# Convolution weights shared between VectorE and GpSimd, and a convolution that begins one tile later in the first image

## The chip, the cores and the metric

The kernel runs on one core of one Trainium2 chip. The metric is the device time of one execution in microseconds (us). Five engines work side by side, each through its own queue in order: TensorE (PE in the profile; its weight loads are PEld), VectorE (DVE), ScalarE (ACT), GpSimd (POOL) and SyncE (SP), which issues most of the transfers. SBUF is the on-chip memory, PSUM the memory into which TensorE accumulates.

## What is computed

Two layers on `x` of 2 images, 256 channels, 64x64, in float32. Layer 0 adds an 8-head attention over all 4096 positions to `x`. Layer 1, which the change touches, adds the following to its input:

```python
x = _gn(x)                                   # group normalisation
q, k, v = (1x1 convolutions of x by conv1, conv2, conv3)
ctx   = _sa(blockify(fq), blockify(fk), blockify(v))     # first attention: 64 tokens of a dilated 8x8 grid
feats = relu(scale * (lr_W @ ctx) + shift)
qx, kx, vx = (two-step 1x1 branches of feats, and sr_fv_w)
ctx2  = _sa(qx, kx, vx)                                  # second attention: 64 tokens of each 8x8 block
out_att = relu(scale * (sr_W @ ctx2) + shift)
f_conv  = fc_w applied over the 12 head slices of q, k, v    # 9 maps for each of 64 head channels
out_conv = grouped 3x3 convolution of f_conv with dep_w
return rate1 * out_att + rate2 * out_conv
```

`f_conv` and the grouped convolution are linear in `x`, so the kernel folds 1x1, mixing and 3x3 into one dense 3x3 convolution from 256 to 256 channels. Its weights depend on the inputs and are made on the chip, once, during the first image.

## The kernel before, in words

The images go one after the other. For each: statistics and projections of layer 0 (`project0`), its attention (`attention0`, some 950 us), the first attention of layer 1 (`layer1_first`) and the second attention together with the convolution (`layer1_second`). Each of the last two runs over NT = 8 tiles of 512 positions.

**Weights of the 3x3 (`conv_weights`, L760 to L840).** It is called at the end of `layer1_first` in the first image, and its instructions are filled in between those of the first attention's tiles. Small factors `weff` come first (L788 to L808). Then, for each half m of the output channels: 12 slices `wx` of 128x256 are loaded (L812); for each of the 9 taps, 12 products of a slice with a column of `weff` are added up (L813 to L820), all on VectorE; from the nine tap sums four rows of four (16 positions) are made by sums and differences (L824 to L831, the weight transform of Winograd's method); each of the 16 goes out to memory as `wf_kept` (L833). `wx`, the tap sums and the new rows lie in one buffer, and `new_cols` (L770) lies on the first eight slices of `wx`, so the second half's `wx` is loaded only when the first half is through. `fetch_conv_weights` (L845) reads all 16 positions back (L848), and in the first image turns each block on TensorE (L857), scales it (L860 on ScalarE, L862 on VectorE) and keeps the result for the second image (L863), which only loads it.

**Second attention and convolution (`layer1_second`, L1146 to L1242).** A tile has a branch for q (`fq1`, `fq2`: `phq_sr`, `prq_sr`), one for k (`phk_sr`, `prk_sr`), the group attention (`pvs_sr` values, `sp_sr` scores, the softmax L985 to L992 on VectorE and ScalarE, `at_sr` transposes, `bd` copies L1006, `pc_sr` context) and the result `res_sr`. The convolution has 16 steps, four for each of four strips of two tiles. A step is `conv_transform` on GpSimd (one instruction L884 and four L888, made one step ahead), 32 matmuls into `mm` (L898), and `conv_step`'s sums on VectorE into the tile's `x` (L904 to L925). TensorE's order is that of the program (`manual_schedule`). The program puts convolution steps at three places of a tile: between the branches, inside the softmax, and at the end of the tile. Before, tiles 0 and 1 have three steps, tiles 2 to 6 two, tile 7 none; `wf` is fetched in tile 0, after the branch for q. When the four steps of a strip are done, its two tiles' results are added up (L1237) and go out (L1240); only then is the `x` buffer free for the next image. The other engines' orders are set by a planner from its own estimates of costs, where the program's order is the priority; buffers of the pool `w4` (11 of them) are handed out the same way.

The choice of places in the code before:

```python
                if t == 0:
                    wf = fetch_conv_weights(b)
                if t + 1 < NT:
                    conv()
...
                if t < 2:
                    conv()
```

Of the kernel before, what the change touches and what calls it, by code (L numbers as in the profile page):

```python
# [17 lines left out]
P = 128  # L18
B, C, H, W = 2, 256, 64, 64
N = H * W  # L20
T = 512
NT = N // T
# [18 lines left out]
def direct_layers(ctx: ExitStack, tc: tile.TileContext, a: dict, out: bass.AP, bad: bass.AP):  # L41
# [3 lines left out]
    nc = tc.nc  # L45
# [13 lines left out]
    def w4(shape, name, dtype=F32):  # L59
        return work.tile(shape, dtype, tag="w4", name=name)  # L60
# [699 lines left out]
    def conv_weights():  # L760

        n_prep = 2 * 81 + 108 + 24 + 4 * 108
        place = vpool.tile([P, UW * C * KC], F32, tag="vw", name="prep")
        prep, rest = place[:, :n_prep], place[:, n_prep : n_prep + 27 * C].rearrange("p (i c) -> p i c", c=C)
        wx, taps, new_rows = rest[:, 0:12], rest[:, 12:21], rest[:, 21:27]
        new_cols = rest[:, 0:8].rearrange("p (r j) c -> p r j c", j=2)  # L770

        def part(at, n):
            return prep[:, at : at + n], at + n

        dep, at = part(0, 2 * 81)
        fcb, at = part(at, 108)
        bx, at = part(at, 24)
        weff, at = part(at, 2 * 108)
        tmp, at = part(at, 2 * 108)
        nc.gpsimd.dma_start(out=dep.rearrange("p (m f) -> p m f", m=2), in_=a["dep"].rearrange("(m p) f -> p m f", p=P))  # L780
        nc.gpsimd.dma_start(out=fcb, in_=a["fc"].partition_broadcast(P))
        nc.gpsimd.dma_start(out=bx.rearrange("p (m i) -> p m i", m=2), in_=a["bx"].rearrange("(m p) i -> p m i", p=P))
        dep = dep.rearrange("p (m o t) -> p m o t", m=2, o=9)
        fcb = fcb.rearrange("p (o i) -> p o i", o=9)
        bx = bx.rearrange("p (m i) -> p m i", m=2)
        weff = weff.rearrange("p (m i t) -> p m i t", m=2, i=12)
        tmp = tmp.rearrange("p (m i t) -> p m i t", m=2, i=12)
        for m in range(2):  # L788
            for o in range(9):
                dst = weff if o == 0 else tmp  # L790
                nc.vector.tensor_tensor(
                    dst[:, m],
                    dep[:, m, o, :].unsqueeze(1).to_broadcast([P, 12, 9]),
                    fcb[:, o, :].unsqueeze(2).to_broadcast([P, 12, 9]),
                    ALU.mult,
                )
                if o:
                    nc.vector.tensor_add(weff[:, m], weff[:, m], tmp[:, m])

        nc.vector.tensor_scalar(  # L800
            weff.rearrange("p m i t -> p (m i t)"), weff.rearrange("p m i t -> p (m i t)"), wts["rate2"], None, ALU.mult
        )
        btap = const.tile([P, 2, 9], F32, name="btap")
        for m in range(2):
            nc.vector.tensor_tensor(
                tmp[:, m], weff[:, m], bx[:, m, :].unsqueeze(2).to_broadcast([P, 12, 9]), ALU.mult
            )
            nc.vector.tensor_reduce(btap[:, m, :], tmp[:, m].rearrange("p i t -> p t i"), AX.X, ALU.add)  # L808

        for m in range(2):  # L810
            for q in range(3):
                nc.gpsimd.dma_start(out=wx[:, 4 * q : 4 * q + 4, :], in_=a["wx"][q, m].rearrange("i p c -> p i c"))  # L812
            for tap in range(9):  # L813
                acc = taps[:, tap, :]
                for i in range(12):
                    src, s = wx[:, i, :], weff[:, m, i, tap : tap + 1]
                    if i == 0:
                        nc.vector.tensor_scalar(acc, src, s, None, ALU.mult)
                    else:
                        nc.vector.scalar_tensor_tensor(acc, src, s, acc, ALU.mult, ALU.add)  # L820

            one, two = new_rows[:, 0:3, :], new_rows[:, 3:6, :]
            g = [taps[:, 3 * dy : 3 * dy + 3, :] for dy in range(3)]
            nc.vector.tensor_add(one, g[0], g[2])  # L824
            nc.vector.tensor_sub(two, one, g[1])
            nc.vector.tensor_add(one, one, g[1])
            for r, row in enumerate((g[0], one, two, g[2])):
                one, two = new_cols[:, r, 0, :], new_cols[:, r, 1, :]
                nc.vector.tensor_add(one, row[:, 0, :], row[:, 2, :])
                nc.vector.tensor_sub(two, one, row[:, 1, :])  # L830
                nc.vector.tensor_add(one, one, row[:, 1, :])  # L831
                for q, src in enumerate((row[:, 0, :], one, two, row[:, 2, :])):
                    nc.sync.dma_start(  # L833
                        out=wf_kept[:, :, 4 * r + q, m * P : (m + 1) * P], in_=src.rearrange("p (k c) -> p k c", k=KC)
                    )
        edges = const.tile([P, 2, 5], F32, name="edges")
        nc.vector.tensor_reduce(edges[:, :, 0], btap, AX.X, ALU.add)
        for e, three in enumerate((slice(0, 3), slice(6, 9), slice(0, 7, 3), slice(2, 9, 3))):
            nc.vector.tensor_reduce(edges[:, :, 1 + e], btap[:, :, three], AX.X, ALU.add, negate=True)
        return btap, edges  # L840
# [32 lines left out]
    def conv_transform(b, xp, s, q):  # L873

        def cols(d):
            return xp[:, :, 16 * s : 16 * s + 18, d : d + W - 1 : 2]

        def rows(d):
            return col[:, :, d : d + 15 : 2, :]

        terms = ((0, 2, False), (1, 2, True), (2, 1, False), (1, 3, False))
        col = cpool.tile([P, KC, 18, W // 2], F32, tag="col", name=f"col_{b}_{s}_{q}")
        one, two, plus = terms[q]
        (nc.gpsimd.tensor_add if plus else nc.gpsimd.tensor_sub)(col, cols(one), cols(two))  # L884
        v = [w4([P, 2, KC, STRIP], f"v_{b}_{s}_{q}_{n}") for n in range(2)]
        for r, (one, two, plus) in enumerate(terms):
            dst = v[r // 2][:, r % 2].rearrange("p k (i j) -> p k i j", j=W // 2)
            (nc.gpsimd.tensor_add if plus else nc.gpsimd.tensor_sub)(dst, rows(one), rows(two))  # L888
        return v
# [135 lines left out]
    def bn_relu(dst, src, col, m):  # L1025
        nc.scalar.activation(  # L1026
            dst, src, AF.Relu, bias=vecs[:, col + 2 + m : col + 3 + m], scale=vecs[:, col + m : col + m + 1]
        )


    def layer1_first(b, xts, put, check, st):
# [109 lines left out]
        if b == 0:  # L1141
            with tc.issue_after(done.ins):
                kept["bias"] = conv_weights()
        return feats, mean, rstd, shift

    def layer1_second(b, xts, feats, mean, rstd, shift, pacc):  # L1146
# [7 lines left out]
        def to_image(t):  # L1154
            for k in range(KC):
                nc.scalar.activation(  # L1156
                    xp[:, k, 1 + 8 * t : 9 + 8 * t, 1 : 1 + W], xts[t][:, k, :].rearrange("p (r w) -> p r w", w=W),
                    AF.Identity, bias=shift[:, k : k + 1], scale=rstd[:, k : k + 1],
                )
# [5 lines left out]
        ahead = {0: conv_transform(b, xp, *turns[0])}  # L1165
        done = 0

        def conv():
            nonlocal done
            if done + 1 < len(turns):  # L1170
                ahead[done + 1] = conv_transform(b, xp, *turns[done + 1])
            conv_step(b, xts, wf, ahead.pop(done), *turns[done], pacc)
            done += 1

        for t in range(NT):
# [25 lines left out]
            with tc.manual_schedule(engines={mybir.EngineType.PE}):  # L1201
                q = branch("fq1", "fq2", V_FQ1, V_FQ2, "q")
                for tt in {0: (3, 4)}.get(t, (t + 4,)):
                    if tt < NT:
                        to_image(tt)
                if t == 0:
                    wf = fetch_conv_weights(b)
                if t + 1 < NT:
                    conv()
                k = branch("fk1", "fk2", V_FK1, V_FK2, "k")  # L1210
                res = w4([P, KC, T], f"res_{nt}")

                def to_res(m, pc, res=res):

                    bn_relu(
                        res[:, m, :].rearrange("p (d o e) -> p o d e", d=8, o=8),
                        pc.rearrange("p (o d e) -> p o d e", o=8, d=8), V_SRW, m,
                    )

                parts = group_attention(  # L1220
                    nt, q, k, lambda c, w, f=f: f[c][:, w * P : (w + 1) * P], wts["fv"], to_res, apart=t + 1 < NT
                )
                next(parts)
                if t + 1 < NT:
                    conv()
                next(parts)
                next(parts, None)
                if t < 2:
                    conv()
            conv_edges(xts, t)  # L1230
            if b == B - 1 and t == 2:
# [594 lines left out]
```

## Time and profile before

| | value |
|---|---|
| time, median of 3 runs | 3211.84 us (3209.8 to 3215.32) |
| span of the profiled execution | 3211.4 us |
| TensorE busy | 3093.3 us, 96% |
| VectorE busy | 2487.2 us, 77% |
| ScalarE busy | 2316.5 us, 72% |
| GpSimd busy | 826.7 us, 26% |
| tap sums L820, 198 instructions on VectorE | 0.479 us each (median), from 1191.1 to 1313.8 us |
| first attention of the first image, TensorE | to some 1312 us |
| second attention and convolution of the first image | 1314 to some 1635 us |

A line of the timeline reads: start and length in us, engine, line of the code, operation, output and inputs, shape, count; in brackets, the idle time of the engine in front of it and what ended it. A group of equal instructions in a row stands as one line. Stages are read from the busy time of each engine in a stretch, given as engine busy time with the number of instructions.

### The profile page before, as it was taken

To read this page: it belongs to the slowest core of one execution; us is meant where nothing else is said; L and a number is where in the kernel's file an instruction comes from. 1 tells how busy PE (TensorE), PEld (TensorE's weight loads), DVE (VectorE), ACT (ScalarE), POOL (GpSimd) and SP (SyncE) were. 2 spreads that over 40 slices of the span, in tenths; PEclk is the share of its full clock that TensorE was granted. 3 is DMA by queue.
4 is the path that set the end of the run, shared out by engine and by line. 5 is a ranking of instruction groups with operands and counts; after the bars stand their busy time and mean duration, and the time that the engine had idled before them with its cause. 6 is when DMAs were issued, how large, how long until landed. Compare 5 with 4: busy or idle time off the path is not lost. (4 is left out here: it accounts for less than half of the span.)

```text
span 3211.4 us, 62287 instructions
## 1 busy us (share of the span) xinstructions
PE 3093.3 (96%) x24889; PEld 1838.3 (57%) x24889; DVE 2487.2 (77%) x3223; ACT 2316.5 (72%) x2371; POOL 826.7 (26%) x918
## 2 busy tenths in 40 slices
PE   7899999999999989699998999999999999899998
PEld 4455555555555545466754555555555555456766
DVE  4599998999999988664445899889999999724543
ACT  2699999999999963422235999999999999724222
POOL 2122222222222210344200222222222222104530
PEclk9999999999999999899999999999999999999999
DMA  7968789689786741310049696897887966500000
GB/s 255 258 132 170 157 156 182 138 166 175 155 178 130 149 101 50 131 33 27 27 174 270 129 183 139 159 173 144 172 168 159 191 130 129 143 3 11 20 14 21
DMA packets 242957, 425.73 MB, mean 133 GB/s; under 512 B 99009, under 2 KB 110361, under 8 KB 240225
## 3 DMA queue, kind: packets, MB, share of 16 engines
q0 software_dynamic: 96176, 240.42, 39.0%
q1 hardware_dynamic: 146480, 181.25, 21.0%
q8 instruction: 197, 3.23, 0.4%
q14 instruction: 104, 0.84, 0.1%
HBM read 118.78 MB, written 67.86 MB: 58 GB/s over the span
## 5 line engine op out<-in xcount | busy, mean ns | idle before, releaser
L519 DVE TENSOR_TENSOR e<-e,es 128x1024 f32<-128x1024 f32 (+1 forms) x952 | 1035.9, 1142 | 96.9 <-ACT es L472 95.1
L482 PE MATMUL av<-es,v 128*32 128x256 f32 (+1 forms) x9644 | 747.6, 390 | 0.0
L519 DVE TENSOR_TENSOR e<-e,v 128x1024 f32<-128x1024 f32 (+1 forms) x640 | 675.9, 1108 | 54.4 <-ACT v L472 53.0
L472 ACT ACTIVATE es<-sa 128x1536 f32<-128x1536 f32 (+1 forms) x444 | 635.6, 1432 | 94.9 <-PE sa L466 54.2
L466 PE MATMUL sa<-q,k 128*128 128x512 f32 x1736 | 561.2, 430 | 13.0 <-issue 4.5
L482 PE MATMUL av<-v 128*32 128x256 f32 (+1 forms) x6228 | 506.9, 389 | 0.0
L482 PEld LDWEIGHTS av<-es,v 128*32 128x32 f32 x9644 | 316.5, 109 | 299.7 <-issue 161.3
L466 PEld LDWEIGHTS sa<-q,k 128*128 128x128 f32 x1736 | 280.0, 188 | 296.5 <-issue 142.4
L466 PE MATMUL sc<-q,k 128*128 128x512 f32 x1180 | 372.3, 397 | 10.1 <-ACT es L472 8.5
L466 PE MATMUL sb<-q,k 128*128 128x512 f32 x1180 | 371.1, 395 | 1.3 <-ACT es L472 1.3
L482 PEld LDWEIGHTS av<-v 128*32 128x32 f32 x6228 | 216.7, 109 | 179.3 <-issue 82.2
L472 ACT ACTIVATE es<-sc 128x1024 f32<-128x1024 f32 x296 | 306.9, 1037 | 7.8 <-DMA v<-es 7.8
L472 ACT ACTIVATE v<-sc 128x1024 f32<-128x1024 f32 x294 | 304.8, 1037 | 1.0 <-DMA acc<-v 1.0
L472 ACT ACTIVATE es<-sb 128x1024 f32<-128x1024 f32 x296 | 302.1, 1021 | 4.0 <-DMA acc<-es 3.9
L472 ACT ACTIVATE v<-sb 128x1024 f32<-128x1024 f32 x294 | 300.0, 1020 | 0.5 <-DMA acc<-v 0.5
L466 PEld LDWEIGHTS sc<-q,k 128*128 128x128 f32 x1180 | 210.3, 188 | 82.4 <-ACT es L472 21.0
L466 PEld LDWEIGHTS sb<-q,k 128*128 128x128 f32 x1180 | 221.0, 188 | 56.1 <-ACT es L472 3.5
L472 ACT ACTIVATE v<-sa 128x1536 f32<-128x1536 f32 (+1 forms) x146 | 209.2, 1433 | 35.0 <-PE sa L466 14.9
L898 PE MATMUL mm<-v,wf 128*128 128x256 f32 x1024 | 229.5, 382 | 3.7 <-DVE z L907 3.7
L529 POOL DMA_DIRECT2D es<-es x118 | 101.2, 858 | 484.8 <-ACT es L472 438.2
L888 POOL TENSOR_TENSOR v<-col 128x512 f32<-128x512 f32 x128 | 162.7, 1300 | 237.2 <-PE sp_sr L977 82.3
L898 PEld LDWEIGHTS mm<-v,wf 128*128 128x128 f32 x1024 | 194.4, 191 | 38.4 <-issue 7.7
(243 smaller groups left out, 3254.2 us busy)
## 6 DMA issues: line engine op xcount, KB each, us to landing
acc<-es POOLq DMA_DIRECT2D x130, 512.0 KB, 6.4
acc<-v POOLq DMA_DIRECT2D x84, 512.0 KB, 6.3
es<-es POOLq DMA_DIRECT2D x138, 256.0 KB, 4.3
v<-es POOLq DMA_DIRECT2D x134, 256.0 KB, 5.1
k<-wk_halves SPq DMA_DIRECT2D x64, 512.0 KB
q<-wq_halves SPq DMA_DIRECT2D x256, 128.0 KB
v<-v POOLq DMA_DIRECT2D x90, 256.0 KB, 5.0
es<-v POOLq DMA_DIRECT2D x86, 256.0 KB, 4.0
```

What stands on the lines that cost most here:

```text
L466: nc.tensor.matmul(sc[:, i, :], held["k", g // 2][:, j * P : (j + 1) * P], held["q", g, u // 2][:, u % 2, :], start=True, stop=True,)
L472: nc.scalar.activation(dst, sc[:, i : i + m, :], AF.Exp, scale=SC0)
L482: nc.tensor.matmul(dst[HD0 * u : HD0 * u + HD0, n], lhs, rhs(u)[:, n], start=start, stop=stop)
L519: nc.vector.tensor_add(dst[:, s, :], dst[:, s, :], src)
L529: nc.gpsimd.dma_start(out=dst, in_=src, accum_op=ALU.add)
L888: (nc.gpsimd.tensor_add if plus else nc.gpsimd.tensor_sub)(dst, rows(one), rows(two))
L898: nc.tensor.matmul(mm[:, m, r, :], wf[:, k, 4 * r + q, m * P : (m + 1) * P], v[r // 2][:, r % 2, k, :], start=k == 0, stop=k == KC - 1,)
```

## The change

Two things. First, of the nine taps in a half, three (6, 7 and 8, the last row of the 3x3) are made on GpSimd, as a product into a scratch row and an addition for each of the 12 slices, where VectorE has one instruction for both; VectorE keeps six. The aim is to have both engines at the sums at once and the weights ready earlier. Second, in the first image no convolution step stands in tile 0 of the second attention; tiles 1 to 4 have three, tiles 5 and 6 two, and `wf` is fetched in tile 1. The aim is to give TensorE work of the attention while the weights aren't there. The second image keeps its order.

```diff
-            for tap in range(9):
-                acc = taps[:, tap, :]
+
+            for tap in (6, 0, 1, 7, 2, 3, 8, 4, 5):
+                acc, term = taps[:, tap, :], new_rows[:, 0, :]
                 for i in range(12):
                     src, s = wx[:, i, :], weff[:, m, i, tap : tap + 1]
-                    if i == 0:
+                    if tap >= 6:
+                        nc.gpsimd.tensor_mul(acc if i == 0 else term, src, s.to_broadcast([P, C]))
+                        if i:
+                            nc.gpsimd.tensor_add(acc, acc, term)
+                    elif i == 0:
                         nc.vector.tensor_scalar(acc, src, s, None, ALU.mult)
                     else:
                         nc.vector.scalar_tensor_tensor(acc, src, s, acc, ALU.mult, ALU.add)
...
+        steps = (0, 3, 3, 3, 3, 2, 2, 0) if b == 0 else (3, 3, 2, 2, 2, 2, 2, 0)
+
...
-                if t == 0:
+                if t == steps.index(max(steps)):
                     wf = fetch_conv_weights(b)
-                if t + 1 < NT:
+                if steps[t] > 0:
                     conv()
...
-                if t + 1 < NT:
+                if steps[t] > 1:
                     conv()
                 next(parts)
                 next(parts, None)
-                if t < 2:
+                if steps[t] > 2:
                     conv()
```

## The prediction

> **What bounds the kernel now.** I went from the busy time by slices (TensorE is at 96% over the span, with one hole near 1330 us) to the stages of that hole, then to the waits in it, then to the timelines of the three engines around it. Busy time by stage (length; PE, PEld, DVE, ACT, POOL; granted clock; DMA share, GB/s):
>
> ```profile
> 1190.60:1245.50 54.90, 54.49 (x311) 33.43 (x311) 51.41 (x142) 22.12 (x32) 0.00 (x0) 1.00 0.05 15
> 1260.40:1314.30 53.90, 50.77 (x278) 30.63 (x276) 51.61 (x136) 24.08 (x35) 0.79 (x6) 1.00 0.12 37
> 1314.30:1331.40 17.10, 7.40 (x16) 2.88 (x16) 17.06 (x12) 11.09 (x17) 15.34 (x10) 0.87 0.22 65
> 1331.40:1346.00 14.60, 0.00 (x1) 0.01 (x1) 0.00 (x0) 0.00 (x0) 10.19 (x7) 0.50 0.79 310
> ```
>
> The first two rows are the tap sums of output half m=0 and m=1: VectorE is nearly full, GpSimd idle, and TensorE is full with the first attention. Row three: VectorE ends the row and column sums (L824 to L831). Row four: the last piece goes out and all weights come back (L848), and TensorE does nothing. The timeline and the wait list of TensorE:
>
> ```profile
> 1318.51 3.70 PE L1194 MATMUL prq_sr<-hq_sr,wt_fq 128*128 128x512 f32 x8 [0.37 <-ACT hq_sr L1026]
> 1346.00 2.40 PE L857 MATMUL pw<-ident,wf 128*128 128x128 f32 x10 [23.79 <-DMA wf<-wf_kept]
> PE pw L857 <- DMA wf<-wf_kept: 23.8, 1, 23.8
> ```
>
> So in the first image TensorE, which sets the end, stands for 23.8 us on a chain: taps m=0, store, reload of `wx` (1245.5 to 1260.4; `new_cols` lies on `wx[0:8]`, so m=1 can't be loaded earlier), taps m=1, sums, store and load (14.6). A later end of that chain moves the rest of the kernel one for one.
>
> **What the skill says.** The Trainium skill, "SBUF — State Buffer", section "Who interferes with whom": VectorE and GpSimd share one port pair under an exclusive lock; a VectorE instruction with two SBUF inputs contends with a GpSimd instruction that reads SBUF, and the loser fully blocks. The tap step L820 has two SBUF inputs (`wx` and `acc`). The trace agrees, where the sums of m=1 meet the convolution's transforms:
>
> ```profile
> 1316.36 2.36 DVE L830 TENSOR_TENSOR prep<-prep 128x256 f32<-128x256 f32 x1
> 1318.65 2.03 DVE L826 TENSOR_TENSOR prep<-prep 128x768 f32<-128x768 f32 x1
> 1320.60 2.89 DVE L829 TENSOR_TENSOR prep<-prep 128x256 f32<-128x256 f32 x2
> 1327.10 4.26 DVE L831 TENSOR_TENSOR prep<-prep 128x256 f32<-128x256 f32 x3
> ```
>
> ```profile
> 1315.82 2.62 POOL L884 TENSOR_TENSOR col<-xp 128x1152 f32<-128x1152 f32 x1 [6.03 <-ACT xp L1156]
> 1318.52 6.09 POOL L888 TENSOR_TENSOR v<-col 128x512 f32<-128x512 f32 x4
> 1326.97 5.50 POOL L888 TENSOR_TENSOR v<-col 128x512 f32<-128x512 f32 x4
> 1368.01 4.93 POOL L888 TENSOR_TENSOR v<-col 128x512 f32<-128x512 f32 x4 [26.19 <-issue]
> ```
>
> A sum of 128x256 takes 0.42 us alone (one each 0.335) and here 1.4 to 2.4: exactly one gets through per GpSimd instruction. GpSimd loses little: four of 128x512 take 4.93 us alone (one each 1.22) and 5.50 beside VectorE, 0.15 more each, some 0.19 less than the VectorE instruction's own pace.
>
> **The change, part by part.**
>
> (a) *Taps 6, 7, 8 to GpSimd.* VectorE loses 3 x 12 instructions per half: 36 x 0.397 = 14.3 us (L820 repeats every 0.397 us: six take 2.46). GpSimd gains 3 x (12 products + 11 sums) = 69 instructions of 128x256 per half. None of that size is in the trace. From below: half of 1.22 is 0.61, and 2.6 cycles an element at 1.2 GHz ("GPSIMD Engine Reference", "3.1 Elementwise — side-by-side cycle accounting") give an estimate of 0.56. From above: the straight line through 512 elements (1.22) and 1152 (2.13, 2.2 from start to start) gives 0.84. I take 0.63: at 512 elements that page's rate gives 1.11, near the 1.22. Every product and sum reads SBUF, so it alternates with L820: a cycle is 0.63 - 0.19 + 0.40 = 0.84 us, in which each engine does one instruction.
>
> Half m=0: VectorE has 66 sums, 6 products and 4 normalisations (L992), 76 contending instructions. About 17% of its time goes to work of the first attention that doesn't contend (maximum, subtraction, sum, reciprocal, two copies: 2.0 us of each 16.0 us tile, and short waits); then GpSimd runs alone. GpSimd: (0.83/0.84 + 0.17/0.63) T = 69, T = 54.9 us. VectorE has done 54 by then; the other 22 take 22 x 0.397/0.83 = 10.4. Half m=0 takes 65.3 us instead of 54.9: **10.4 us longer**, although 14.3 us of VectorE's work is gone.
>
> Half m=1 starts at 1270.8. To 1309 the first attention is still there: 48 of GpSimd's 69; the other 21 take 17.6, to 1326.6. VectorE has then done 59 of 74; 15 and the 15 row and column sums are left. Now GpSimd, whose queue is in order, comes to the convolution's transforms (three turns of L884 and 4 x L888 and one more L884, as before: 16 instructions, 23.4 us alone, some 26 so). VectorE gets 16 through by 1352.6, the other 14 take 5.8: the chain ends at **1358.4, not 1331.4: D = 27 us later**. Store and load (14.6) stay.
>
> (b) *No convolution in tile 0 of the first image; `wf` fetched in tile 1.* TensorE's stay moves behind tile 0's second branch and attention and tile 1's first branch. That work, today after the wait: 7.0 (k branch from 1362.35), 3.0 (values, scores), 4.4 (transposes, values, context), 7.2 (q branch): 21.6 us, now done while it would stand. New: the softmax of tile 0 isn't hidden by a convolution step.
>
> ```profile
> 1371.04 1.15 PE L977 MATMUL sp_sr<-rk_sr,rq_sr 128*64 128x64 f32 x32
> 1372.12 7.17 PE L898 MATMUL mm<-v,wf 128*128 128x256 f32 x32
> 1379.13 0.38 PE L997 MATMUL at_sr<-ident,e_sr 128*128 128x128 f32 x2
> ```
>
> Scores end at 1372.2, VectorE is through with L992 at 1375.4: 3.3 us of standing. Without other waits TensorE would be ready for the weights at 1322.2 + 21.6 + 3.3 = 1347.1; they come at 1346 + D. For D over 1.1 the time is 3211.8 - 21.6 + D.
>
> (c) *Queues.* The softmax of tile 0 can land on VectorE behind blocked tap sums; even behind the last of them, 4 us of chain, 4.5 of TensorE and the 7.2 of the q branch end within 2 us of the weights' arrival (14.6 after it), so up to 2 us. The convolution steps number 16 as before; from tile 4 on the two orders have done the same number (12, 14, 16). Tiles 3 and 4 now have three steps where tiles 0 and 1 had them: 42 us of TensorE each against some 34 of VectorE, hidden. Three results instead of two are held to tile 2's first step, in 11 `w4` buffers: nothing to 2 us. In the first attention a softmax chain of 3.5 us grows to 7 with 8.1 of TensorE's work beside it: hidden or covered by the wait for the weights. The second image keeps its order: nothing.
>
> Sum: 3211.8 - 21.6 + 27.0 = 3217.2, say 3217 us.
>
> **Rivals.**
> 1. *GpSimd runs beside VectorE.* Then a half ends after 54.9 - 14.3 = 41 us on VectorE and 69 x 0.63 = 43 on GpSimd, the chain some 24 us earlier, and the weights are there before 1347: TensorE saves 23.8 - 3.3 and the slow clock of the transposes (10 take 2.40 at 1346, later 8 take 0.87: 2.6 us): 3189. For it: L820 never stands beside a GpSimd instruction in the trace. Against: L919, the same operation, does, and two of 128x128, 0.6 us alone, took 3.56 us at 1385.25, one for each GpSimd instruction. A milder form (cycle 0.75, GpSimd 0.56) gives D = 17 by the same steps: 3207.
> 2. *GpSimd at 0.84 alone, 1.05 in turn.* Half m=0 takes 80 us, GpSimd ends m=1 at 1356, the sums at 1385: D = 54, 3244, slower by 1%. For it: the straight line through two sizes. Against: those rows run over two and three dimensions, a tap is one flat row.
> 3. *Transforms put between the taps on GpSimd's queue* (the planner picks by its own estimates): up to 7 us a turn, 3224 to 3231. The taps come first in the program, which speaks against it.
>
> **How the numbers follow.** The alternation at 0.75 to 0.95 us a cycle: 0.5, 3207 to 3231, middle 3217. Rival 1 whole or in good part: 0.25, 3189 to 3205. Rivals 2 and 3: 0.25, 3224 to 3244. The range 3190 to 3242 leaves out the ends. Faster by over 0.2% (below 3205.4): rival 1 and the edge of the middle, 0.32. Within 0.2%: 0.27. Slower: 0.41.
>
> **What would show it.** L820 repeating at 0.8 to 0.9 us while GpSimd works, not 0.397; GpSimd's products at about 0.63; half m=0 ending near 1256; the sums near 1358; TensorE standing some 25 us before L857 with tile 0's attention ahead of it. Wrong, if L820 keeps 0.4 us, if the last sum ends before 1335, or if TensorE's stay is under 10 us.

## The result and the profile after

The changed kernel takes 3236.9 us (median of 4 runs, 3234.5 to 3238.3) where the kernel before, on the same chip, takes 3210.8: a ratio of 1.0078, with an interval of 1.006 to 1.0095. It is slower, by 0.8%. The profiled span is 3236.4 us, 25.0 over the 3211.4 of before.

Lines of the code have moved: a tap sum is now L825 on VectorE (L823 its first product), and L819 (product) and L821 (addition) on GpSimd; the softmax is L990 to L997, its transposes L1002, the `bd` copies L1011, the context L1020, the stores of the weights L838, the transposes of the weights L862.

Busy time by stage of the kernel after (length; PE, PEld, DVE, ACT, POOL with their counts; granted clock; DMA share, GB/s). The rows are GpSimd's taps of m=0, its taps of m=1, the last sums, and the way of the weights to memory and back:

```profile
1190.50:1245.20 54.70, 42.26 (x211) 24.25 (x212) 54.58 (x81) 14.53 (x21) 49.76 (x69) 0.84 0.03 9
1265.20:1320.60 55.40, 40.09 (x174) 22.60 (x172) 55.24 (x80) 11.84 (x18) 50.40 (x69) 0.85 0.05 16
1320.60:1332.60 12.00, 9.40 (x17) 3.45 (x17) 11.72 (x29) 3.15 (x6) 0.00 (x0) 0.72 0.33 93
1332.60:1347.20 14.60, 14.60 (x84) 9.15 (x84) 2.73 (x8) 5.79 (x9) 0.00 (x0) 1.00 0.87 332
```

In the last row the weights come in, at the time they came before (1347.2 against 1346.0), and TensorE is full and doesn't care. In the first two it is not: in the first it works 42.3 us of 54.7, where before it was full to 0.4 us, and it gets 211 matmuls done where it had done 311. The timeline of TensorE, and its waits from 1190 to 1360 us:

```profile
1229.55 0.69 PE L1002 MATMUL at_lr<-ident,e_lr 128*128 128x128 f32 x2 [5.75 <-DVE e_lr L997]
1240.01 3.47 PE L1020 MATMUL pc_lr<-bd,vs_lr 128*128 128x128 f32 x16 [3.95 <-DVE bd L1011]
...
1299.14 0.69 PE L1002 MATMUL at_lr<-ident,e_lr 128*128 128x128 f32 x2 [5.62 <-DVE e_lr L997]
1303.89 3.78 PE L1077 MATMUL pk_lr<-xg,wt_w 128*128 128x512 f32 x4
...
1323.20 0.79 PE L1081 MATMUL pq_lr<-loc_lr,st_posq 16*128 16x512 f32 x1 [5.83 <-DMA loc_lr<-loc_kept]
...
1381.65 0.44 PE L1002 MATMUL at_sr<-ident,e_sr 128*128 128x128 f32 x2 [2.62 <-DVE e_sr L997]
...
1394.06 7.15 PE L862 MATMUL pw<-ident,wf 128*128 128x128 f32 x64
```

```profile
PE at_lr L1002 <- DVE e_lr L997: 16.0, 4, 5.8
PE pc_lr L1020 <- DVE bd L1011: 8.5, 3, 4.0
PE pq_lr L1081 <- DMA loc_lr<-loc_kept: 5.8, 1, 5.8
```

The wait of 23.8 us for `wf` is gone: the weights' transposes have no bracket. In its place TensorE waits 30.3 us inside the **first attention**, 24.5 for VectorE and 5.8 for a load. The rest of that attention's delay, some 16 us, is the same matmuls taking longer: 670 of them keep TensorE busy for 136.3 us (1191.6 to 1359.3), and for 120.2 in the kernel before (1190.6 to 1312.3). Four projections into `pk_lr` take 3.78 us at 1303.89, and 1.98 where nothing stopped TensorE. The Trainium skill, "TensorE: Matmul & The Clock Gate", "Part 1: The HAM clock gate", says that the array goes to half its clock after an idle window of some 3.4 us. The halving agrees: seven stretches with a granted clock of 0.50 to 0.53 hold 32.7 us of TensorE's work, and half of that, an estimate of what the lower clock cost, is the 16 us. The length doesn't agree: after a stop of only 2.33 us, to 1204.46, the granted clock was 0.50 from 1205.7 to 1212.0. In all the first attention ends near 1359 us instead of 1312.

VectorE between the first and the second softmax in the changed kernel, and then the start of the second softmax in the kernel before, where VectorE stood ready and waited for the scores:

```profile
1204.33 4.94 DVE L825 SCALAR_TENSOR_TENSOR prep<-prep 128x256 f32<-128x256 f32 x6
...
1211.63 3.25 DVE L825 SCALAR_TENSOR_TENSOR prep<-prep 128x256 f32<-128x256 f32 x4
1214.80 0.70 DVE L823 TENSOR_SCALAR prep<-prep 128x256 f32<-128x256 f32 x1
1215.42 9.13 DVE L825 SCALAR_TENSOR_TENSOR prep<-prep 128x256 f32<-128x256 f32 x11
1224.58 0.42 DVE L990 TENSOR_REDUCE nm_lr<-sp_lr 128x4 f32<-128x256 f32 x1
```

```profile
1209.09 0.42 DVE L985 TENSOR_REDUCE nm_lr<-sp_lr 128x4 f32<-128x256 f32 x1 [0.37 <-PE sp_lr L977]
```

After the change TensorE finished the scores at 1215.7. VectorE takes their maximum at 1224.58, when the eleven tap sums that stand ahead of it in its queue are through. The number of tap instructions between one softmax and the next is fixed when the kernel is built. From the first softmax on it is 32, 30, 5 (where the row and column sums stand), 33 and 32; in the kernel before, too, most places had 30 to 33. At 0.40 us each 32 fit in a tile of 16.0 us, at 0.82 they take 26. The softmaxes begin at 1197.1, 1224.6, 1248.8, 1266.2, 1294.3 and 1321.3 us: a tile takes 27.5, 24.2, 17.4, 28.1 and 27.0 us, not 16.0. The tap sums by tile (shortest, median and longest in ns), after and then before:

```profile
L825 DVE SCALAR_TENSOR_TENSOR prep<-prep x132: 472/830/1023, 1193.1 to 1325.8; 128x256 f32<-128x256 f32 x132
```

```profile
L820 DVE SCALAR_TENSOR_TENSOR prep<-prep x198: 453/479/487, 1191.1 to 1313.8; 128x256 f32<-128x256 f32 x198
```

The last weight sum is at 1332.6 us (1331.4 before), so VectorE's 72 fewer instructions bought nothing for the weights, and the slower ones hold up all that shares VectorE's queue.

### The profile page after: what moved, and what is told of

It reads as the page before. It is cut to its first block, busy times and chain, and to the rows that moved or that the text cites. A ratio compares the mean times of both kernels' runs of the same rounds, so it can differ in the third digit from the quotient of the medians.

```text
span 3236.4 us, 62356 instructions
## 1 busy us (share of the span) xinstructions
PE 3109.4 (96%) x24889; PEld 1846.5 (57%) x24889; DVE 2508.2 (77%) x3151; ACT 2314.8 (72%) x2371; POOL 926.5 (29%) x1056
## 5 line engine op out<-in xcount | busy, mean ns | idle before, releaser
L472 ACT ACTIVATE v<-sa 128x1536 f32<-128x1536 f32 (+1 forms) x146 | 209.2, 1433 | 35.8 <-PE sa L466 13.8
```

The costliest lines, as they stand in the source:

```text
L472: nc.scalar.activation(dst, sc[:, i : i + m, :], AF.Exp, scale=SC0)
```

## The experiments

**Theory A:** beside GpSimd's reads a tap takes twice as long, and what the kernel loses is lost in queues whose order is fixed, with the first attention's softmax behind tap sums. The new convolution order by itself brings what the prediction's part (b) says. **Theory C** is the prediction: the weights come late. **Theory D:** any GpSimd work slows VectorE. **Theory E:** VectorE has no time for both kinds of work beside GpSimd, whatever their order. B and F are each named in the one expectation that needs them.

### Each part alone

`e1_order_only`: the taps as before, the convolution order as after.

```diff
-            for tap in (6, 0, 1, 7, 2, 3, 8, 4, 5):
+            for tap in range(9):
...
-                    if tap >= 6:
-                        nc.gpsimd.tensor_mul(acc if i == 0 else term, src, s.to_broadcast([P, C]))
-                        if i:
-                            nc.gpsimd.tensor_add(acc, acc, term)
-                    elif i == 0:
+                    if i == 0:
```

> Part (b) alone: all nine taps on VectorE as before, convolution from tile 1, wf fetched in tile 1. Theory A (the loss is the first attention held up by VectorE's tap sums behind the shared port; the later convolution itself is worth what the prediction said): the first attention ends near 1312 us as before, tile 0 fills the 23.8 us of standing except 3.3 us of softmax, TensorE waits for the weights under 2 us: 3188 to 3192 us. Theory B (the new order of the convolution is what costs): slower than 3212.

Measured: 3190.5 us, ratio 0.9941 (0.9927 to 0.9954). It is the fastest kernel of the study, and beats both. From its timeline of TensorE:

```profile
1332.23 0.44 PE L998 MATMUL at_sr<-ident,e_sr 128*128 128x128 f32 x2 [2.78 <-DVE e_sr L993]
...
1343.38 7.15 PE L858 MATMUL pw<-ident,wf 128*128 128x128 f32 x64
```

The attention of tile 0 fills the 23.8 us of waiting, the softmax laid bare costs 2.78, and the weights are there when TensorE comes to them.

`e2_taps_only`: the taps as after, the convolution order as before.

```diff
-        steps = (0, 3, 3, 3, 3, 2, 2, 0) if b == 0 else (3, 3, 2, 2, 2, 2, 2, 0)
...
-                if t == steps.index(max(steps)):
+                if t == 0:
                     wf = fetch_conv_weights(b)
...
```

> Part (a) alone: three taps on GpSimd, the old places of the convolution steps. Theory A: the first attention ends some 47 us late, near 1359, and the weights are in memory by about 1346, before TensorE has done tile 0's q branch, so there is no standing ahead of L857 and the old order loses nothing against the new: 3230 to 3237 us. Theory C (the prediction's own: the chain of the weights is late by about 27 us and TensorE stands for it): 3238 or more, with over 20 us of standing ahead of L857.

Measured: 3229.9 us, ratio 1.0068 (1.0053 to 1.0084), at the lower edge of what A expected. Its list of TensorE's waits from 1190 to 1366 us:

```profile
PE at_lr L1001 <- DVE e_lr L996: 15.3, 4, 6.6
PE pc_lr L1019 <- DVE bd L1010: 12.9, 4, 4.9
PE pq_lr L1080 <- DMA loc_lr<-loc_kept: 3.6, 1, 3.6
```

There is no wait for `wf` here either, though nothing was moved into its place. So theory C falls: even with the old order the weights are not late; the first attention is later than they are. It also says why the two parts don't add up: the new order fills a hole, and with the taps on GpSimd there is no hole. By medians it is worth 19.2 us alone; on top of the taps it brings nothing, and the changed kernel even lies 26.1 us above its kernel before, this one 20.3. Whether those 5.8 us are real is not shown, since the intervals of the two ratios overlap; in the two profiles the changed kernel starts the second attention 3.6 us later (1360.87 against 1357.25) and has the 2.62 us of its softmax laid bare.

### What makes VectorE slow

`e6_fills`: GpSimd goes on writing SBUF but, except for the first product of each tap, no longer reads it. Its other instructions become fills of two rows (0.53 us each); VectorE's first product becomes a two-input multiplication. Taps 6 to 8 are left out of the result.

```diff
-                        nc.gpsimd.tensor_mul(acc if i == 0 else term, src, s.to_broadcast([P, C]))
-                        if i:
-                            nc.gpsimd.tensor_add(acc, acc, term)
+                        if i == 0:
+                            nc.gpsimd.tensor_mul(acc, src, s.to_broadcast([P, C]))
+                        else:
+                            nc.gpsimd.memset(new_rows[:, 0:2, :], 0.0)
+                            nc.gpsimd.memset(new_rows[:, 0:2, :], 0.0)
                     elif i == 0:
-                        nc.vector.tensor_scalar(acc, src, s, None, ALU.mult)
+                        nc.vector.tensor_mul(acc, src, s.to_broadcast([P, C]))
```

> As e3_pool_writes, with its two flaws mended: each GpSimd tap begins with its product, so nothing starts before the taps, and the fills cover two rows (512 elements, 22 a tap); VectorE's first product of a tap is a two-input product[...]. Taps 6 to 8 of the weights are left out of the result. Theory A (only GpSimd's reads block VectorE's second input): L827 beside the fills stays at 0.40 us, the first attention at 16 us a tile: 3186 to 3195 us. Theory D (any GpSimd work blocks it): 0.8 us or more and 3225 to 3240.

Measured: 3189.9 us, ratio 0.9932 (0.9916 to 0.9949). Its tap sums by tile:

```profile
L827 DVE SCALAR_TENSOR_TENSOR prep<-prep x132: 449/477/831, 1191.2 to 1281.3; 128x256 f32<-128x256 f32 x132
```

```profile
1198.06 2.46 DVE L827 SCALAR_TENSOR_TENSOR prep<-prep 128x256 f32<-128x256 f32 x6
```

The median is that of before, and the scores of the first attention follow each other at 16.03 us. In half m=0 the fills began at 1164.9, so that a part of them was over before the taps; the rest, one every 0.58 us to 1208.5, stood beside them, and six taps at 1198.06 took 2.46 us, as before. In half m=1 they stood beside nearly all taps (1245.2 to 1279.0; eleven taps at 1245.43 took 4.43 us). So it is not GpSimd's being busy that doubles a tap but its reading. That is what the Trainium skill, "SBUF — State Buffer", "Who interferes with whom", says of a VectorE instruction with two SBUF inputs: it contends with a GpSimd instruction that reads, not with one that only writes. That both read the same buffer isn't needed: in the kernel before, the sums (`prep`) and the transforms (`col`) met in the same way, in the lines that the prediction shows.

The run says one thing more. VectorE has 36 instructions fewer in a half here than in `e1_order_only`, each at its old pace, and the time is the same (3189.9 and 3190.5 us, ratios 0.9932 and 0.9941 with overlapping intervals). With the new order TensorE waits for `wf` in neither, so even a division that cost VectorE nothing had nothing left to gain.

`e3_pool_writes` was the first form of this: fills of one row (0.33 us, one every 0.25), VectorE's first product left as `tensor_scalar`, taps 6 to 8 left out as well.

```diff
-                        nc.gpsimd.tensor_mul(acc if i == 0 else term, src, s.to_broadcast([P, C]))
+                        nc.gpsimd.memset(acc if i == 0 else term, 0.0)
                         if i:
-                            nc.gpsimd.tensor_add(acc, acc, term)
+                            nc.gpsimd.memset(acc, 0.0)
```

> The changed kernel with each product and sum of GpSimd replaced by a fill with zeros of the same row, so GpSimd is as often busy and writes SBUF but reads none of it; taps 6 to 8 of the weights are then left out of the result. VectorE's order is instruction for instruction that of the changed kernel. Theory A (VectorE's second SBUF input waits for GpSimd's reads): the tap sums on VectorE are back at 0.40 us each, the first attention at 16 us a tile, weights early: 3186 to 3193 us. Theory D (any GpSimd work, its writes or its semaphores, or the order on VectorE itself holds things up): 3215 to 3237.

Measured: 3208.3 us, ratio 0.9994 (0.9984 to 1.0003): neither answer. The taps took 0.40 us, as A has it, but the fills had nothing to wait for and began at 1167.7, beside earlier work of VectorE, and in half m=1 this happened on VectorE:

```profile
1251.99 13.01 DVE L823 TENSOR_SCALAR prep<-prep 128x256 f32<-128x256 f32 x2 [6.16 <-DMA prep<-in_wx_dram]
```

Two products of 0.35 us took 13 us, until the fills were over. The same section says that `tensor_scalar` can enter a mode that uses both port pairs, and that VectorE then contends with GpSimd. The run agrees, together with `e6_fills`, where that product has two inputs and the fills leave the taps alone; that the product was in this mode is not shown apart from its length.

### One tap instead of three

`e8_one_tap`: only tap 8 on GpSimd.

```diff
-            for tap in (6, 0, 1, 7, 2, 3, 8, 4, 5):
+            for tap in (8, 0, 1, 2, 3, 4, 5, 6, 7):
...
-                    if tap >= 6:
+                    if tap >= 8:
```

> One tap (8) on GpSimd instead of three, eight on VectorE, the new order of the convolution. Theory A: GpSimd works 23 x 0.81 = 19 us in each half, in which VectorE's taps lose 23 x 0.43 = 10 us; of that some 5 us a half are in the slack of the first attention, so it ends about 10 us late, near 1322: 3194 to 3206 us, a third of the way or less from 3190 (no tap) to 3237 (three). Theory F (a cost of having taps on GpSimd at all, such as the waits between the engines): nearer to 3237 than to 3190.

Measured: 3200.8 us, ratio 0.9965 (0.9953 to 0.9978). Two tiles of the first attention, those at the start of a half, take 20.4 and 23.0 us, the tile after the second 17.1, the others 16.0. With the new order and 0, 1 and 3 taps on GpSimd the kernel takes 3190.5, 3200.8 and 3236.9 us, so theory F falls. Less of it is only less of a loss.

### Is it the order of the queues?

`e4_paced`: the changed kernel, with each of VectorE's taps held behind the `bd` copies of a given tile, so that about 16 stand in a tile, not 32.

```diff
+                    with paced(m, 12 * tap + i):
+                        if i == 0:
+                            nc.vector.tensor_scalar(acc, src, s, None, ALU.mult)
+                        else:
+                            nc.vector.scalar_tensor_tensor(acc, src, s, acc, ALU.mult, ALU.add)
...
+    bd_copies = []
+
+    def paced(m, n):
+        tile_before = (n - 10) // 16 if m == 0 else min(5 + (n - 8) // 16, NT - 1)
+        return tc.issue_after(bd_copies[tile_before]) if tile_before >= 0 else nullcontext()
...
+        bd_copies.append(copied.ins)
```

> The changed kernel, all work as in it, but VectorE's tap instructions are put behind the bd copies of given tiles, so that some 16 stand between two softmaxes of the first attention where the planner put up to 33. Theory A with the fixed order as the cause: the tap sums still take 0.8 us, but the first attention keeps 16 to 17 us a tile and ends by 1320; the weights come later instead, between 1360 and 1375, as the prediction reckoned: 3203 to 3222 us. Theory E (the port alone costs TensorE this time, whatever the order): 3230 to 3240.

Measured: 3243.1 us, ratio 1.0105 (1.0089 to 1.012): a miss. Its waits of TensorE, and then of VectorE:

```profile
PE at_lr L1010 <- DVE e_lr L1005: 19.8, 3, 18.9
PE pq_lr L1090 <- DMA loc_lr<-loc_kept: 15.0, 2, 14.7
PE at_sr L1010 <- DVE e_sr L1005: 13.1, 1, 13.1
```

```profile
DVE prep L831 <- POOL prep L821: 24.3, 2, 13.7
```

Scores followed each other at 16.0 us where the taps were spread (1260.30, 1276.34, 1292.37, 1308.39). But the row sum L831, which needs GpSimd's taps, now stood ahead of the rest of a softmax on VectorE's queue and waited there, 10.6 us before the L831 at 1243.4 alone.

`e5_paced_sums`: the same, with the sums and stores of a half behind VectorE's last tap of that half.

```diff
+                            final = nc.vector.scalar_tensor_tensor(acc, src, s, acc, ALU.mult, ALU.add)
+
+            with tc.issue_after(final.ins):
+                one, two = new_rows[:, 0:3, :], new_rows[:, 3:6, :]
...
```

> The paced kernel with one more order: the row and column sums of a half stand behind the half's last tap on VectorE, so that they can't wait for GpSimd's taps in front of a softmax (24.3 us of that in e4_paced). All work as in the changed kernel. Theory A with the fixed order as the cause: tap sums at 0.8 us, the first attention at 16 to 17 us a tile and done by 1322; the last weight sum between 1345 and 1365, TensorE stands 8 to 30 us ahead of the transposes of the weights: 3203 to 3225 us. Theory E (shared port alone, in any order, costs the first attention its time): 3230 or more.

Measured: 3238.2 us, ratio 1.0081 (1.0064 to 1.0098): a miss in the total again. Its waits of TensorE, and then of SyncE:

```profile
PE pq_lr L1091 <- DMA loc_lr<-loc_kept: 15.4, 1, 15.4
PE phq_sr L1203 <- DMA wt_fq<-in_fq_dram: 9.9, 1, 9.9
PE at_sr L1011 <- DVE e_sr L1006: 8.2, 1, 8.2
PE at_lr L1011 <- DVE e_lr L1006: 7.5, 4, 5.0
```

```profile
SPq L841 <- POOL prep L821: 124.5, 4, 34.5
```

The waits for VectorE in the first attention are 8.5 us (`at_lr` 7.5, `bd` 1.0) where the changed kernel has 24.5, beside taps with a median of 0.83 us. The loss had moved to the next queue in order: the weights' stores wait on SyncE for GpSimd's taps, and the loads of `loc_lr` and `wt_fq`, which need nothing of the taps, stand behind them.

`e9_paced_stores` takes those stores off SyncE's queue; `e10_stores` does this alone, without pacing.

```diff
-                    nc.sync.dma_start(
+                    nc.gpsimd.dma_start(
                         out=wf_kept[:, :, 4 * r + q, m * P : (m + 1) * P], in_=src.rearrange("p (k c) -> p k c", k=KC)
```

> As e5_paced_sums, with one edit: the 16 stores of a half's weights (L841) are issued on GpSimd's queue instead of SyncE's, where in e5_paced_sums they stood for 124.5 us of waiting ahead of the loads of loc_lr (TensorE waited 15.4) and of wt_fq (9.9). Theory A (what the change costs is what stands behind slow tap work in queues whose order is fixed when the kernel is built: VectorE's first, and with that mended SyncE's): both waits go. The chain of the weights does not move much (last sum near 1365 to 1377 in e5_paced_sums), so part comes back as a wait for wf: 3210 to 3228, under e5_paced_sums' 3238 by 10 or more, and the first attention's tiles at 16 to 17.5 us throughout. Theory E (beside GpSimd's reads VectorE has no time for taps and softmax together; queues only show it): the waits move to at_lr, at_sr or wf in full, 3233 to 3243.

> The changed kernel with one edit: the stores of the weights (L838) go on GpSimd's queue instead of SyncE's. TensorE's wait of 5.8 us for loc_lr at 1323 goes; those for VectorE (at_lr 16.0 over 4, bd 8.5 over 3) stay, since VectorE's order is nearly the same. Theory A: 3228 to 3234, tiles of the first attention still at 24 to 28 us where 32 taps lie in one. Theory E says the same of this run; it is here as the fellow of e9_paced_stores.

Measured for `e9_paced_stores`: 3224.5 us, ratio 1.0037 (1.0023 to 1.0051), 13.8 less than `e5_paced_sums` (from another series, whose ratio was 1.0081) and inside what A expected of the time. Of the tiles of the first attention two are over A's 17.5 us, at 18.0 and 20.4. The branch for q of the second attention starts at 1326.1 us, 34.8 before that of the changed kernel (1360.9). What is left, by its waits of TensorE and the timelines of VectorE and GpSimd:

```profile
PE at_sr L1011 <- DVE e_sr L1006: 19.7, 1, 19.7
PE at_lr L1011 <- DVE e_lr L1006: 10.0, 4, 4.2
```

```profile
1334.03 11.09 DVE L827 SCALAR_TENSOR_TENSOR prep<-prep 128x256 f32<-128x256 f32 x8
...
1355.91 0.42 DVE L999 TENSOR_REDUCE nm_sr<-sp_sr 128x4 f32<-128x256 f32 x1
...
1357.94 6.13 DVE L1006 TENSOR_TENSOR e_sr<-e_sr,den_sr 128x256 f32<-128x256 f32 x1
```

```profile
1336.62 5.54 POOL L896 TENSOR_TENSOR v<-col 128x512 f32<-128x512 f32 x4
...
1358.48 6.70 POOL L896 TENSOR_TENSOR v<-col 128x512 f32<-128x512 f32 x4
```

The taps that were put off now meet the convolution's transforms, eight of them in 11.09 us, and the softmax of tile 0 comes after them and after the half's sums, to be blocked itself. This is the collision that the prediction had foreseen for the changed kernel. So theory E is right in one thing: three taps on GpSimd leave VectorE too little room. One softmax (2.0 us) and 16 taps at 0.82 make 15.1 of a tile's 16.0, and there are two halves' sums besides. Order explains most of the loss in the first attention, 34.8 of 46.4 us by the start of that branch (1314.4 in the kernel before); but what it saved there came back in part as the 19.7 us above, and no order tried here made the division pay.

Measured for `e10_stores`: 3243.1 us, ratio 1.0093 (1.0076 to 1.011), above the 3228 to 3234 expected. The wait for `loc_lr` (5.8) went, and those for VectorE grew by 10.3, from 24.5 to 34.8:

```profile
PE at_lr L1002 <- DVE e_lr L997: 24.8, 6, 8.2
PE pc_lr L1020 <- DVE bd L1011: 10.0, 5, 3.3
```

Its weights are turned from 1394.3 us, as in the changed kernel (1394.1), so the load that came earlier brought nothing while VectorE's queue set the pace. I had subtracted a wait that hid behind another. The first matmul after the second attention of this image starts at 1661.6 us there and at 1662.0 in the changed kernel; the 5 us more of its span come later, in stages that the edit doesn't touch (32 matmuls into `p_wk` take 16.99 us at 1666, and 15.59 in the changed kernel). Why they do is open.

## Why the prediction was right and wrong

The forecast was 3217 us, 3190 to 3242, with slower the likeliest of three at 0.41. The time lies in the range, 20 us above the point, and for the most part by luck: the 27 us of late weights that carried the sum did not come, and a delay of some 47 us in the first attention, which the sum had at nothing, did. The mechanism of part (a) was right; the place where it does harm was not.

- **(a), the alternation**: right. GpSimd does an instruction every 0.81 us (a product of 0.68 and a sum of 0.79 each 1.62), against the 0.84 worked out; a tap on VectorE has a median of 0.83. GpSimd's half took 54.7 us (54.9 predicted), the second 55.4 (55.8); so close an agreement is in part chance, since a shorter cycle made up for the time alone that GpSimd did not get. VectorE's last tap of m=0 ended at 1251.4, not 1256; VectorE had no pauses (54.6 us busy of 54.7) in which GpSimd could have run ahead.
- **(a), D = 27 us**: wrong, measured 1.2 (last weight sum 1332.6 against 1331.4). The 15 sums were to meet the convolution's transforms on GpSimd. They didn't: the transforms need `xp`, whose fill waits for the last values of the first attention, and GpSimd began it at 1356.1. The sum left out that the first attention, by then some 47 us late, would hold off the transforms. The collision itself exists; `e9_paced_stores` has it.
- **(b), the new order**: right. 21.6 us of work went ahead of the weights; the softmax laid bare cost 2.62 (2.78 in `e1_order_only`) where 3.3 was worked out. The weights' 64 transposes took 7.15 us at full clock, 9.61 before: 2.5 us that rival 1 counted and the main sum did not. In `e1_order_only` the profiled span was 24.6 us shorter, 2.5 of them ahead of the first scores, and the median 19.2 below that of the kernel before.
- **(c), the step that failed**: "a softmax chain of 3.5 us grows to 7 with 8.1 of TensorE's work beside it: hidden or covered by the wait for the weights". The chain did grow to 7.3 us (1197.1 to 1204.4). But the step counted only the instructions of the softmax, not those ahead of them. I took the taps for filling that gives way to a softmax as soon as its scores are there. They are a fixed sequence, placed when the kernel is built, some 32 between two softmaxes, as many as when a tap took 0.40 us. 32 x 0.42 us more makes 13 us; the tiles with 30 or more taps grew by 8 to 12. Nor could a wait for the weights cover it: it lies before that wait and took its place.

The balance closes. TensorE was to be ready for the weights at 1347.1 and to get them at 1373; it was ready at 1394.1, and they had come by 1347.2. 1394.1 - 1373 - 2.5 (the clock of the transposes) = 18.6 of the 19.7 us by which the point was low. Against the kernel before: 48.1 (the transposes' start, 1346.0 to 1394.1) - 21.6 - 2.5 = 24.0 of the 25.0 in the span.

The prediction's own signs say the same. "TensorE standing some 25 us before L857" did not come, and two of those that were to show it wrong did: the last sum ended before 1335 (1332.6), and TensorE's stay for the weights was under 10 us (none). And the dense TensorE of the first attention, which I had read as a bound, had no reserve: VectorE was full beside it (51.4 of 54.9 us) and in its queue.

## What to carry to other kernels

When an instruction gets slower, look at what stands behind it on its engine, not only at what it makes: an order fixed at build time keeps its counts, so filling that was sized for 0.4 us delays everything after it when it takes 0.8. Before giving part of VectorE's two-input work to GpSimd, see whether GpSimd would read SBUF: here each instruction of the one then waited for one of the other, and 36 instructions fewer in 108 did not pay for the other 72 at twice the time. See also whether the work to be shortened still holds anything up once the order is changed; here it didn't. Change order and division apart from each other; here the half that filled TensorE's wait with other work was worth 0.6%, and the other half ate it and more.

## What the runs showed of the hardware that was not expected

- One tile's softmax scaling of 128x256 (0.42 us alone) took 6.13 us beside four GpSimd additions of 128x512 and, at first, stores that GpSimd was issuing (`e9_paced_stores`), and two `tensor_scalar` of 0.35 us took 13 us beside fills one every 0.25 us (`e3_pool_writes`). The alternation of one for one, seen with the taps, is not a promise: by these durations VectorE lost several times in a row. What decides that was not tested.
- GpSimd's product of 128x256 takes 0.68 us and its sum 0.79 beside VectorE. The three products at the start, one after the other while VectorE is for the most part at other work, take 1.80 together.
- Short stops were dear on TensorE: 30.3 us of waits in the first attention, of 1 to 6 us each, came with some 16 us more of delay, as matmuls at a granted clock of 0.50, where it had been 1.00. After a stop of 2.33 us it was 0.50 for 6 us; after that of 5.62 us before 1299.14 it was still 0.50 at 1307, 8 us into the work.
